# One scan over two states in a layer-0 Mamba scan, with the work around it moved

## The chip, the cores and the metric

The kernel runs on one NeuronCore of a Trainium2 chip, in one launch. The metric is the time of an execution on the device in microseconds (us). A core has a matrix engine (PE, with its weight loads shown as PEld), a vector engine (DVE), a scalar engine that evaluates functions (ACT), a general one (POOL) and DMA queues; each works through its own list of instructions in order and waits for the others by semaphores. All data here are 32-bit floats. [...]

## The reference

Four layers on an input of 2 x 256 x 48 x 48 (two batches of 2304 tokens, 256 channels). The first is a bidirectional Mamba layer, and the change is nearly all in it:

```python
def _selective_scan(u, delta, A, Bm, Cm, D):
    h0 = jnp.zeros((Bsz, d, A.shape[1]), u.dtype)
    def step(h, xs):
        d_t, B_t, C_t, u_t = xs
        dA = jnp.exp(d_t[..., None] * A)
        h = dA * h + (d_t * u_t)[..., None] * B_t[:, None, :]
        y = jnp.einsum('bdn,bn->bd', h, C_t)
        return (h, y)
    _, ys = lax.scan(step, h0, xs)
    return ys.transpose(1, 0, 2) + u * D

def _mamba_branch(xi, z, ...):
    xs = silu(conv4(xi) + conv_b)               # causal, per channel
    proj = xs @ xproj_w.T                       # 16 for dt, 16 B, 16 C
    dt = softplus(proj[..., :16] @ dtproj_w.T + dtproj_b)
    A = -exp(A_log)
    return _selective_scan(xs, dt, A, Bm, Cm, D) * silu(z)

h = layernorm(seq, ln_g, ln_b) + pos
xi, z = split(h @ in_proj_w.T)                  # 512 channels each
y = branch_f(xi, z) + flip(branch_b(flip(xi), flip(z)))
x = seq + y @ out_proj_w.T
```

So for each of 512 channels and each of 16 states there is a recurrence over 2304 tokens, in both directions, for two batches. Layer 1 is x + block(groupnorm(x)) with a linear attention, a depthwise convolution and an MLP. Layer 2 is an attention with 3 heads, where a head embeds tokens with `W_embed[h]` (768 x 256) and the heads' outputs go through `W_out` (256 x 768), then a graph-gated mixture of four experts. Layer 3 is an attention with sigmoid and a mixture of eight experts. Layers 2 and 3 normalise their tokens first.

## The kernel before

Channels lie on the partitions. The stream `E.xres` (128 x 2 x 4608) stays in SBUF over all layers. `layer0` cuts the 2304 tokens of a batch into 6 pieces of W = 384 and works through `order`: for each batch 6 pieces forward, then 6 backward, 24 in all. The 512 channels are DB = 4 blocks of 128.

For a piece, `prepare` makes what the scan needs: the 4-tap convolution as matmuls with diagonal weights (L266) with a copy out by ACT (L270), Silu (L276; in backward pieces also Silu of z, L278), the projection to dt, B and C (L286), which goes through DRAM as `bcd`, and dt as the softplus relu(v) + ln(1 + exp(-|v|)) with a correction for the rounding of 1 + e (L299 to L312). It ends with `dtu` = dt u on POOL (L314).

`scan` is the heart. For two channel blocks at a time and a group of GN = 4 states, B and C rows are loaded to all partitions (`bb`, `cc`, L354 and L356), POOL makes `db` = dt u B for the group and one block (128 x 1536, L359), and then for each state

- ACT computes exp(A dt) into a PSUM bank, tile `hs` (L376), 128 x 384;
- DVE runs the recurrence over it with `tensor_tensor_scan` (L382 forward, L385 backward, with reversed access), starting from `state` (0 in the first piece), in place in PSUM, or into an SBUF tile `ho` where the product goes to POOL;
- DVE (5 of 8) or POOL (3 of 8, `GP`) multiplies by C: `hc` (L390);
- ACT copies the last column to `state` (L392);
- PE adds `hc` to the sum over states by a matmul with the identity into `yp` (L344); products of POOL are added LAG = 4 states later.

PSUM in this stage: five banks for `hs` (tag "hs"), one for all other small products (`hold`, tag "mm"), two for `yp`.

Beside the scans of a piece, every two states, steps of three generators are issued: `project_out` of the piece before (backward pieces; L318 to L328, the last of which adds to `xres`), `prepare` of the next piece, and in pieces 0 to 9 `project_in` (normalisation, Sqrt L185, input projection) of a piece that is needed later. `beside` holds for each the number of its steps and the slot of 32 by which they are to end. What is issued is then put in order for each engine's queue by a scheduler. ACT's functions come from several tables; a change of table is an instruction of its own (ACT_TABLE_LOAD) on the line of the function that needs it.

Layer 1 begins with `group_norm` of batch 0 (L510 to L535): statistics (`bn_stats`, L517) over the stream, a matmul with `gmat` (L520, L528), which averages over groups of 8 channels, Sqrt, reciprocal, and the normalised tokens `xn` (L533); the first matmul with `wqkv` is L547. Layer 2's attention first makes products of weights for each of three heads: `w_eo` holds `W_embed[h]` beside `W_out` (L708, L709); 72 matmuls `pg` (L713) give `gm`, 144 small ones `pu` (L721) give `ub`; then come transposes of the tokens (L741) and the queries `pq` with `gm` (L750).

## Time and profile before

| | |
|---|---|
| median of 3 executions | 5455.18 us (5454.78 to 5460.61) |
| the profiled execution | 5416.49 us |
| its span | 5414.7 us |
| mean granted PE clock | 0.955 of full speed |
| PE / DVE / ACT / POOL busy over the span | 4771.7 / 3503.3 / 2365.8 / 2410.2 us |
| start of the first `dtu` / last scan's stage end | 92.2 / about 2393 us |
| first `pk` of layer 1 | 2417.2 us |
| first `pq` of layer 2 | 3181.6 us |

The profile comes from one execution, which was 0.7% shorter than the median of the three timed ones. A group's row gives line, engine, operation, output and inputs with shapes, the count, then busy time in us and the mean duration of one in ns, then the engine's idle time just before these instructions and what ended it. A timeline's row gives start and duration in us. Consecutive instructions of one engine overlap a little at their ends, so a busy mean is longer than the step from one start to the next.

### The profile page before, as it was taken

The numbers are of one execution on the slowest core, as the hardware profiler recorded it, in microseconds if no ns is written. First come the engines' busy times: TensorE is split into PE (matmuls) and PEld (weight loads), VectorE is DVE, ScalarE is ACT, GpSimd is POOL, SyncE is SP. The second block draws the span as 40 slices with busy tenths as digits, with TensorE's granted clock in tenths as the row PEclk, the third lists the DMA queues.
The fourth block names the chain that finished last, engine by engine and source line by source line (L and its number), as shares of the span: only waits on it lengthen the run. The fifth ranks groups of instructions, "written<-read, shape, count | busy, mean of one in ns | idle before, by whom it ended". The sixth has DMA issues, their size and how long they took to land. (4 is left out here: it accounts for less than half of the span.)

```text
span 5414.7 us, 47212 instructions
## 1 busy us (share of the span) xinstructions
PE 4771.7 (88%) x15246; PEld 2653.7 (49%) x15246; DVE 3503.3 (65%) x5360; ACT 2365.8 (44%) x4935; POOL 2410.2 (45%) x1308
## 2 busy tenths in 40 slices
PE   7888888888877778769999999999999999999897
PEld 3444444443333334335555555556654455555675
DVE  4899898898999898899996234447634401212343
ACT  5767777666667666632222213332123222222111
POOL 3888887788999888860000000008802100000321
PEclk8999999999999889989999989999999999999898
DMA  4445454443545444431110010011122200000422
GB/s 162 163 170 179 161 177 171 156 150 140 172 148 178 152 152 158 146 138 33 40 38 6 0 39 0 27 36 30 22 71 55 61 3 9 6 9 8 84 82 93
DMA packets 178083, 491.28 MB, mean 91 GB/s; under 512 B 32182, under 2 KB 100666, under 8 KB 177562
## 3 DMA queue, kind: packets, MB, share of 16 engines
q1 hardware_dynamic: 169114, 475.36, 25.6%
q0 software_dynamic: 8704, 12.73, 1.6%
q8 instruction: 124, 2.03, 0.2%
q14 instruction: 141, 1.16, 0.1%
HBM read 416.44 MB, written 71.58 MB: 90 GB/s over the span
## 5 line engine op out<-in xcount | busy, mean ns | idle before, releaser
L344 PE MATMUL yp<-hc,ident 128*128 128x384 f32 x3072 | 1203.1, 525 | 291.6 <-DVE hc L390 251.7
L359 POOL TENSOR_TENSOR db<-dtu,bb 128x1536 f32<-128x1536 f32 x384 | 1332.3, 3471 | 49.7 <-issue 19.1
L344 PEld LDWEIGHTS yp<-hc,ident 128*128 128x128 f32 x3072 | 577.1, 199 | 873.5 <-DVE hc L390 447.6
L390 POOL TENSOR_TENSOR hc<-ho,cc 128x384 f32<-128x384 f32 x576 | 579.4, 1014 | 185.3 <-DVE ho L382 83.3
L390 DVE TENSOR_TENSOR hc<-hs,cc 128x384 f32<-128x384 f32 x960 | 498.5, 540 | 39.1 <-PE yp L344 37.8
L376 ACT ACTIVATE hs<-dt,negab 128x384 f32<-128x384 f32 x768 | 434.2, 581 | 93.3 <-DVE ho L385 42.1
L376 ACT ACTIVATE hs<-dt,negaf 128x384 f32<-128x384 f32 x768 | 433.4, 581 | 55.0 <-DVE hc L390 25.5
L385 DVE TENSOR_TENSOR_SCAN hs<-hs,state,db 128x384 f32<-128x384 f32 x400 | 395.1, 1010 | 56.0 <-POOL db L359 30.3
L382 DVE TENSOR_TENSOR_SCAN hs<-hs,state,db 128x384 f32<-128x384 f32 x400 | 396.1, 1010 | 30.2 <-POOL db L359 22.9
L1771 POOL DMA_INDIRECT xe<-xt_d,token x48 | 47.4, 987 | 754.3 <-issue 716.0
L266 PE MATMUL mm<-xw,w_cv 128*128 128x384 f32 x768 | 287.5, 510 | 67.2 <-ACT xs L270 29.4
L1706 PE MATMUL po<-at,xtok 128*128 128x384 f32 x864 | 329.9, 507 | 7.7 <-ACT at L1704 7.5
L912 POOL PARTITION_ALL_REDUCE most<-most x1 | 0.4, 380 | 738.6 <-DVE most L911 738.6
L1697 PE MATMUL sp<-qT,xn 128*128 128x384 f32 x864 | 317.4, 487 | 0.0
L1704 ACT ACTIVATE at<-sp 128x384 f32<-128x384 f32 x216 | 104.6, 490 | 472.7 <-PE sp L1697 472.6
L1354 PE MATMUL ph<-xn,w 128*128 128x384 f32 x768 | 288.2, 519 | 19.3 <-ACT hid L1358 7.6
L627 PE MATMUL pf<-t,wfc 128*128 128x384 f32 x768 | 255.5, 489 | 0.0
L646 PE MATMUL po<-hid,wfc 128*128 128x384 f32 x768 | 253.6, 486 | 0.0
L385 DVE TENSOR_TENSOR_SCAN ho<-hs,state,db 128x384 f32<-128x384 f32 x240 | 240.0, 1000 | 15.2 <-ACT hs L376 15.1
L382 DVE TENSOR_TENSOR_SCAN ho<-hs,state,db 128x384 f32<-128x384 f32 x240 | 239.5, 998 | 8.4 <-ACT hs L376 8.2
L266 PEld LDWEIGHTS mm<-xw,w_cv 128*128 128x128 f32 x768 | 145.9, 196 | 195.1 <-ACT xs L270 46.9
L392 ACT COPY state<-hs 128x1 f32<-128x1 f32 x800 | 117.5, 155 | 278.2 <-DVE hc L390 276.3
(433 smaller groups left out, 7947.6 us busy)
## 6 DMA issues: line engine op xcount, KB each, us to landing
bb<-bcd SPq DMA_DIRECT2D x192, 768.0 KB, 4.1
cc<-bcd SPq DMA_DIRECT2D x192, 768.0 KB, 4.1
xw<-xi_d SPq DMA_DIRECT2D x24, 774.0 KB, 5.3
w<-in_m_w SPq DMA_DIRECT2D x16, 1024.0 KB, 5.8
y_d<-y SPq DMA_DIRECT2D x32, 384.0 KB, 2.3
ye<-y_d SPq DMA_DIRECT2D x32, 384.0 KB, 3.5
xi_d<-xz SPq DMA_DIRECT2D x48, 192.0 KB, 3.0
z_d<-xz SPq DMA_DIRECT2D x48, 192.0 KB, 3.2
```

The costliest lines, as they stand in the source:

```text
L266: nc.tensor.matmul(px, lhsT=w_cv[b, s][:, d * 4 + k, :], rhs=xw[:, d, o : o + W], start=k == 0, stop=k == 3,)
L344: nc.tensor.matmul(yp[d], lhsT=E.ident, rhs=hc, start=False, stop=summed[d] == NS)
L359: nc.gpsimd.tensor_tensor(db, bc(dtu[:, d, :], [P, GN, W], 1), bb, ALU.mult)
L376: nc.scalar.activation(hs, dt[:, d, :], AF.Exp, scale=nega[s][:, d * NS + n : d * NS + n + 1])
L382: nc.vector.tensor_tensor_scan(to, hs, db[:, j], init, ALU.mult, ALU.add)
L385: nc.vector.tensor_tensor_scan(to[:, ::-1], hs[:, ::-1], db[:, j, ::-1], init, ALU.mult, ALU.add)
L390: (nc.gpsimd if on_pool else nc.vector).tensor_tensor(hc, to, cc[:, j, :], ALU.mult)
L627: nc.tensor.matmul(pf, lhsT=wfc1[:, k, f * P : (f + 1) * P], rhs=t1[:, k, :], start=k == 0, stop=k == 1,)
L646: nc.tensor.matmul(po[m], lhsT=wfc2[:, f, m * P : (m + 1) * P], rhs=hid[:, i, :], start=f == 0, stop=f == 15,)
L1354: nc.tensor.matmul(ph, lhsT=w1[:, e, k, f * P : (f + 1) * P], rhs=xn[:, k, c * W : (c + 1) * W], start=k == 0, stop=k == 1,)
L1697: nc.tensor.matmul(sp, lhsT=xn[:, k, t0 + i * P : t0 + (i + 1) * P], rhs=qT[:, k, c * W : (c + 1) * W], start=k == 0, stop=k == 1,)
L1706: nc.tensor.matmul(po[m], lhsT=xtok[:, i, m * P : (m + 1) * P], rhs=at, start=i == 0, stop=i == MT - 1,)
```

## The change

**Two states in one scan.** The tile `hs` becomes two banks (128 x 1024), of which the columns 127 to 896 are used: twice 385 columns, 384 tokens and one leading column each (at the far end in backward pieces). `dt` gets a leading column of BIG = 1e25, so that exp(A dt) is 0 there, and A is kept below -2e-23; `db` gets a leading column too, which holds the state from the piece before (0 in a first piece). At the leading column the recurrence is thus begun anew, 0 times what came before plus the state, and one scan of 770 elements, started from an immediate 0, does two states. The exps stay one for each state, 128 x 385. The product with C is one instruction of 128 x 768 for the pair, on DVE or POOL in the same shares (`at * 3 % 8 >= 5`), the copy of the last columns is one of 128 x 2, and PE adds the two halves by two matmuls as before. The states are copied into `db` by ACT, 128 x 4 for a group. PSUM: two pair tiles `hs`, two banks for `mm`, two for `yp`. LAG is 2 pairs. The SBUF tiles `ho`, `hc` and `hcp` have two buffers of pairs where there were four of single states.

**dt u B mid-group.** `begin_group` issues the loads of `bb` and `cc`, the product `db` and the copy of the states half a group before they are used, also over the border to the next piece.

**dt.** The correction is rewritten, with one ACT instruction fewer for a piece, and `dtu` is four POOL instructions of one block each; `prepare` has 21 steps, to end at slot 29.

**Head products.** The products of layer 2's weights are made by `head_products`, beside the scans of the 12 pieces that follow the last `project_in` (there are 12 units of three steps), in the buffers of `pos`, `h`, `sq` and `rs`, which are free by then; the result goes to DRAM (`gm_d`) and is loaded again at the start of layer 2. `ub` stays in SBUF.

**Group norm.** `gmat` is built at the kernel's start, and `group_stats` of batch 0 runs beside the scans of the piece (1, "f", 1); that of batch 1 stays in layer 1. One normalisation in layer 3 gets a pool of its own.

```diff
-    GP = ((1, 3), (2,))
-    LAG = 4
+    LAG = 2
+    BIG = 1e25
...
-    psh = ctx.enter_context(tc.tile_pool(name="l0ps_h", bufs=5, space=PSUM))
-    ps = ctx.enter_context(tc.tile_pool(name="l0ps_s", bufs=1, space=PSUM))
+    psh = ctx.enter_context(tc.tile_pool(name="l0ps_h", bufs=2, space=PSUM))
+    ps = ctx.enter_context(tc.tile_pool(name="l0ps_s", bufs=2, space=PSUM))
...
-        dt = wp.tile([P, DB, W], F32, tag="dt", name="dt")
+        lead, body = (0, slice(1, W + 1)) if fwd else (W, slice(0, W))
+        dts = wp.tile([P, DB, W + 1], F32, tag="dt", name="dt")
+        nc.vector.memset(dts[:, :, lead : lead + 1], BIG)
+        dt = dts[:, :, body]
...
-        nc.scalar.activation(dtu, dtu, AF.Identity, bias=one[:, 1:2])
...
-        nc.vector.tensor_tensor(ex, ex, dtu, ALU.subtract)
+        nc.vector.scalar_tensor_tensor(ex, dtu, -1.0, ex, ALU.add, ALU.subtract)
         nc.vector.tensor_tensor(dt, dt, ln, ALU.add)
-        nc.vector.tensor_tensor(dt, dt, ex, ALU.add)
+        nc.vector.tensor_tensor(dt, dt, ex, ALU.subtract)
-        nc.gpsimd.tensor_tensor(dtu, dt, xs, ALU.mult)
+        for d in range(DB):
+            nc.gpsimd.tensor_tensor(dtu[:, d, :], dt[:, d, :], xs[:, d, :], ALU.mult)
+            yield
...
+    def head_products():
+        DT, D = 6, 768
+        for h, m, z in [(h, m, z) for h in range(3) for m in range(2) for z in range(2)]:
+            w_eo = []
+            for k in range(3):
+                rows = slice((z * 3 + k) * P, (z * 3 + k + 1) * P)
+                t = up.tile([P, 2, W], F32, tag=("pos", "h", "sq")[k], name="w_eo")
+                t = t.rearrange("p k w -> p (k w)")[:, : 2 * C]
+                nc.sync.dma_start(t[:, 0:C], p["W_embed"][h, rows, :])
+                nc.sync.dma_start(t[:, C:], p["W_outT"][rows, :])
+                w_eo.append(t)
+            yield
+            pg = ps.tile([P, 2 * C], F32, tag="mm", name="pg")
+            for k in range(3):
+                nc.tensor.matmul(
+                    pg, lhsT=w_eo[k][:, m * P : (m + 1) * P], rhs=w_eo[k], start=k == 0, stop=k == 2
+                )
+            if z == 0:
+                part = up.tile([P, 2 * C], F32, tag="rs", name="part")
+                nc.scalar.copy(part, pg)
+            else:
+                nc.vector.tensor_tensor(part, part, pg, ALU.add)
+                nc.sync.dma_start(E.gm_d[h, m], part)
+            yield
...
+    groups = [(d0, g, d) for d0 in range(0, DB, 2) for g in range(NS // GN) for d in (d0, d0 + 1)]
+    held = {}
+    def begin_group(q, first_piece, b, s, c, xs, y, dts, dtu, bcd):
+        d0, g, d = groups[q]
+        if d == d0:
+            for n, o in (("bb", 16), ("cc", 32)):
+                held[n] = wp.tile([P, GN, W], F32, tag=n, name=n)
+                nc.sync.dma_start(
+                    held[n], bcd[o + g * GN : o + (g + 1) * GN, :].partition_broadcast(P)
+                )
+        lead, body = (0, slice(1, W + 1)) if s == "f" else (W, slice(0, W))
+        db = wp.tile([P, GN, W + 1], F32, tag="db", name="db")
+        nc.gpsimd.tensor_tensor(
+            db[:, :, body], bc(dtu[:, d, :], [P, GN, W], 1), held["bb"], ALU.mult
+        )
+        if first_piece:
+            nc.gpsimd.memset(db[:, :, lead : lead + 1], 0.0)
+        else:
+            nc.scalar.copy(db[:, :, lead], state[:, d, g * GN : (g + 1) * GN])
+        return db, held["cc"]
...
+            for j in range(0, GN, 2):
+                n = g * GN + j
+                on_pool = at * 3 % 8 >= 5
+                hs = psh.tile([P, 1024], F32, tag="hs", name="hs")[:, 511 - W : 513 + W]
+                for i in range(2):
+                    o = d * NS + n + i
                     nc.scalar.activation(
-                        hs, dt[:, d, :], AF.Exp, scale=nega[s][:, d * NS + n : d * NS + n + 1]
+                        hs[:, i * (W + 1) : (i + 1) * (W + 1)], dts[:, d, :], AF.Exp,
+                        scale=nega[s][:, o : o + 1],
                     )
...
+                nc.vector.tensor_tensor_scan(
+                    to[:, way], hs[:, way],
+                    db[:, j : j + 2, :].rearrange("p i w -> p (i w)")[:, way], 0.0, ALU.mult, ALU.add,
+                )
+                to = to.rearrange("p (i w) -> p i w", i=2)
+                hc = wp.tile([P, 2, W], F32, tag="hcp" if on_pool else "hc", name="hc")
+                (nc.gpsimd if on_pool else nc.vector).tensor_tensor(
+                    hc, to[:, :, body], cc[:, j : j + 2, :], ALU.mult
+                )
+                if step < NCH - 1:
+                    nc.scalar.copy(state[:, d, n : n + 2], to[:, :, last])
...
+                if j == 0:
+                    if q + 1 < len(groups):
+                        begun = begin_group(q + 1, step == 0, b, s, c, xs, y, dts, dtu, bcd)
+                    elif following:
+                        begun = begin_group(0, step == NCH - 1, *following)
...
-            beside.append((prepare(nb, s2, c2, ready), 15, 25))
+            beside.append((prepare(nb, s2, c2, ready), 21, 29))
         if i < len(pieces):
             beside.append((project_in(*pieces[i]), 12, 32))
+        elif i < len(pieces) + 12:
+            beside.append((islice(heads, 3), 3, 32))
+        if (b, s, step) == (1, "f", 1):
+            beside.append((group_stats(E, up, lambda: hold()[:, 0:2], 0), 15, 32))
```

## The prediction

> **What bounds the kernel now.** I read the page first: its engine table, its 40 slices, and its groups of instructions. In the slices
>
> ```profile
> PE   7888888888877778769999999999999999999897
> ...
> DVE  4899898898999898899996234447634401212343
> ...
> POOL 3888887788999888860000000008802100000321
> ```
>
> slices 2 to 18 (135 us each) are another regime than the rest: DVE is at 8 to 9 tenths and POOL just behind. That is layer 0. After it PE is the bound and this change touches only two spots there. I then took the busy times over the scan stage; the columns are PE, PEld, DVE, ACT, POOL, the clock, the DMA share and GB/s:
>
> ```profile
> 100.00:2393.00 2293.00, 1856.97 (x5000) 918.80 (x5001) 2079.73 (x2684) 1550.77 (x3575) 1960.04 (x984) 0.95 0.46 160
> 1527.20:1616.60 89.40, 71.53 (x193) 33.55 (x192) 86.67 (x108) 61.94 (x155) 82.56 (x41) 0.98 0.45 159
> 1901.10:1997.90 96.80, 78.95 (x210) 40.64 (x210) 87.44 (x118) 65.86 (x157) 82.12 (x43) 0.91 0.43 156
> ```
>
> DVE works 2079.7 of 2293 us (91%), so the stage goes as DVE's work plus DVE's holes: 213 us of holes over 24 pieces, 9 each. The second line is one forward piece of batch 1 (2.7 us of holes), the third a backward one (9.4). POOL works 82 us in each, ACT 62 to 66. What DVE's time is made of, by shape:
>
> ```profile
> L390 DVE TENSOR_TENSOR hc<-hs,cc 128x384 f32<-128x384 f32 x960 | 498.5, 540 | 39.1 <-PE yp L344 37.8
> L382 DVE TENSOR_TENSOR_SCAN hs<-hs,state,db 128x384 f32<-128x384 f32 x400 | 396.1, 1010 | 30.2 <-POOL db L359 22.9 <-ACT hs L376 6.9
> ...
> L382 DVE TENSOR_TENSOR_SCAN hs<-hs,db 128x384 f32<-128x384 f32 x80 | 74.6, 951 | 21.4 <-POOL db L359 16.2 <-ACT hs L376 4.3 <-ACT state L392 0.9
> ...
> L177 DVE TENSOR_TENSOR h<-xres,mm 128x768 f32<-128x768 f32 x12 | 11.4, 947 | 29.6 <-PE mm L176 18.0 <-PE mm L202 11.6
> ...
> L1599 DVE TENSOR_TENSOR_SCAN run<-ones,before,tot 128x18 f32<-128x18 f32 x8 | 1.4, 247 | 0.0
> ```
>
> Busy times overlap at the ends, so I price by the step from start to start in DVE's timeline. A table change on ACT (here for the Silu of z) stands in ACT's timeline, and what DVE lost to it in DVE's:
>
> ```profile
> 2236.28 0.58 ACT L376 ACTIVATE hs<-dt,negab 128x384 f32<-128x384 f32 x1
> ...
> 2237.38 1.28 ACT L278 ACT_TABLE_LOAD   x1
> 2238.67 1.49 ACT L278 ACTIVATE y<-y 128x1536 f32<-128x1536 f32 x1
> ...
> 2241.16 1.28 ACT L376 ACT_TABLE_LOAD   x1
> 2242.45 0.58 ACT L376 ACTIVATE hs<-dt,negab 128x384 f32<-128x384 f32 x1
> ```
>
> ```profile
> 2230.57 1.01 DVE L385 TENSOR_TENSOR_SCAN ho<-hs,state,db 128x384 f32<-128x384 f32 x1
> 2231.49 1.00 DVE L385 TENSOR_TENSOR_SCAN hs<-hs,state,db 128x384 f32<-128x384 f32 x1
> ...
> 2238.45 1.02 DVE L385 TENSOR_TENSOR_SCAN hs<-hs,state,db 128x384 f32<-128x384 f32 x1 [0.49 <-POOL db L359]
> 2239.39 1.47 DVE L390 TENSOR_TENSOR hc<-hs,cc 128x384 f32<-128x384 f32 x3
> 2243.07 1.02 DVE L385 TENSOR_TENSOR_SCAN hs<-hs,state,db 128x384 f32<-128x384 f32 x1 [2.21 <-ACT hs L376]
> ```
>
> A scan takes a step of 0.915; three products take 1.47, so one 0.46 by steps (busy 0.54). ACT began no exp from 2236.28 to 2242.45, 6.2 us; DVE, with up to five exps in store, lost 2.2 of them.
>
> **Paired scans.** A pair on DVE is now 2 x 0.915 + 2 x 0.46 = 2.75; a pair whose product goes to POOL costs DVE 2 x 0.915 = 1.83. The paired scan has 770 elements and an immediate start. Between the scan of 18 (247 ns, L1599) and that of 384 (1010) an element costs (1000-247)/366 = 2.06 ns; from 951 for the immediate form the pair is 951 + 386 x 2.06 = 1746, and less the 95 ns by which steps overlap 1.65. The product pair is the 768 form of L177: 947, a step of 0.865 by one overlap of 0.08. So a DVE pair costs 2.52 and saves 0.23, a POOL pair saves 0.175. There are 24 x 32 = 768 pairs, 480 and 288: 110 + 50 = 160. In the four first pieces the scans already start from an immediate and save 0.11 less on 128 pairs: 14. Together **-146**, 6.1 a piece. Bounds: a pair at 2 x 0.915 takes 134 of it back; at the slope of the scans of 384 read down to 1.9 ns an element it gives 50 more.
>
> **Two pair buffers where five banks were.** That is the price. The store in front of DVE falls to one pair, 1.65 to 2.52 us of work, and the exps of pair k+2 wait for the product (or, for POOL pairs, the scan) of pair k. A burst is 1.28 + 1.48 + 1.28 = 4.04, and then two exps (0.58 each) and a state copy before the next scan: 5.2 between two pairs. Walking ACT's and DVE's queues of the changed order with these durations, in a backward piece of batch 1: Silu of z falls between the two exps of one pair, DVE stands 5.2; Silu of xs 3.2; Abs and Relu 1.2; Exp and Identity 0.4; Ln 0.4; sum 10.4 where 9.4 stand: +1.0. Forward batch 1, whose holes are 2.7, has no Silu of z, so Silu of xs and part of the rest: +1.5. With project_in's Sqrt beside (pieces 1 to 9) a hole of about 3 more: forward batch 0 +5.7, backward batch 0 +3. Six pieces of each: 6 x 11.2 = **+67**. Below, -100: the holes now charged to POOL db (74 in the waits) and to yp could go, since db is begun half a group earlier. Above, +322: three full bursts a piece, 15.6, less the 2.2 that DVE now waits for ACT's exps (52 in its waits over 24 pieces), 13.4 a piece. I take the walk, as it is nearest to the real order, but I walked some twenty pairs of 768.
>
> **What else is in the pieces.** DVE gets the bn_stats of batch 0 (12 of 0.55, step 0.46, and eight small ones) +7; the head products' adds (6 of 128x512 at 0.69 and 18 small at 0.2) +8 to 10; the start of layer 0, with two tiles instead of five and the dtu in four, +3: **+20**. ACT loses an Identity of 1.57 per piece and gains 16 state copies of 0.19 in front of db; they wait for the last scan of the older db, which lies behind on DVE, so cost exps at most 0.2 each. POOL: 16 db of 3.47, 12 product pairs of 1.90 (the 128x768 product of L1412 on POOL, mean 1897), four dtu of about 1.0: 82.3 a piece, as before; a forward piece of 89.4 - 6.1 + 1.5 = 84.8 still lies above it. PE takes 72 pg (512 columns, 0.52 each) and 144 pu, 61 us, at 81% use: hidden, and if each head unit held up the conv matmuls on their two banks by 1 us, +12. SP issues 72 weight loads and 6 stores more, in a stage at 46% of DMA; bb and cc are issued half a group early, ahead of the head loads. If SP held them back a group by 2 us once a piece, +24.
>
> **Layer 2's start.** In PE's timeline the first head matmul starts at 3118.1, the last ends at 3178.6 and the first pq is at 3181.6:
>
> ```profile
> 3118.14 5.25 PE L721 MATMUL pu<-vec,w_eo 128*128 128x1 f32 x24 [2.50 <-DMA w_eo<-in_W_embed]
> ...
> 3170.79 7.82 PE L721 MATMUL pu<-vec,w_eo 128*128 128x1 f32 x48
> ...
> 3181.60 6.38 PE L750 MATMUL pq<-xn,gm 128*128 128x384 f32 x16
> ```
>
> Without them pq comes when the last norm (its last matmul runs 3123.25 to 3124.9) and the transposes beside it are through, about 3124.5: **-57** (-63 to -50). The gm reload (three loads, 1.57 MB) can be issued early and is about the size that lands in 6 us (w, 1 MB, 5.8); uncovered it costs those 6.
>
> **Layer 1's start.** From the last xres add (2398.75) to the first pk (2417.16) are 18.4 us: mask, stats, two small matmuls, xn. With batch 0's statistics done only xn (2.85) and the load of wqkv (landing 4.7 after) stay, about 8: **-10** (-13 to -8).
>
> **Sum:** -146 + 67 + 20 - 57 - 10 = -126, on an execution of 5416.5 (span 5414.7, 1.8 around it). That execution lies 38.7 (0.7%) under the median of 5455.2; I apply the difference to the median: **5330**.
>
> **A rule against it.** In the burst above the Silu starts 1.29 after its load started, and the load lasts 1.28: nothing more lies between. The Trainium skill's "ScalarE: Activation LUTs", section "What ACT_TABLE_LOAD costs", gives 1283 ns for a load and about 1380 more for a drain, 2.66 per switch. With one pair in store every such drain would fall on DVE: by that page an estimate of three bursts of two switches in 24 pieces, 199 us more, and the change would be slower, about 5530. The row decides: no drain.
>
> **Rivals.** (A) *The two buffers starve DVE.* Each burst stalls it nearly whole. For: ACT's bursts are three a piece, and today's 2.2 in the burst shown was lost with five banks. Against: my walk, where the store of one pair still covers half. It decides when a piece gets over 193/24 = 8.0 us more holes (193 = 146 + 57 + 10 - 20); halfway to the bound of 13.4, at 10.7, it ends 5455 - 193 + 257 = **5519** (5584 at the bound). (B) *No more holes than today*, because the early db removes the 74 us of db waits: 5455 - 193 = **5262**; POOL's 82.3 x 24 = 1975 does not yet forbid that. (C) *The scans gain nothing*, since new holes of 6.1 a piece eat the 146: only heads, layer 1 and the +20 stay, 5455 - 47 = **5408**. A pair that costs two single scans, with the walk's holes, would be 5330 + 134 = 5464, about no change.
>
> **How the numbers follow.** Chances: forecast 0.50 (own range 5290 to 5375), B 0.13, C 0.15, A 0.19, and 0.03 that gains and stalls meet within 0.2%, about what a measurement of this kernel can tell from no change. Faster 0.78, slower 0.19. The range 5240 to 5470 takes in B, C and the near end of A; it leaves out the rest of A, some 0.15, and 0.04 below.
>
> **What would show it.** Scans of 128x770 at about 1.75 and products of 128x768 near 0.95 on DVE; DVE at 1.95 ms busy in a scan stage near 2240; its holes charged to ACT hs, no longer to POOL db; the longest near 5 where Silu of z runs; POOL at 82 a piece. First pq some 57 earlier against the end of layer 1, first pk 8 after the last xres add. Wrong if: the pair costs over 1.8, ACT's waits exceed 10 a piece in all four kinds of piece, a queue that I called free (SP, PE's two banks) shows up as releaser, or layer 2 waits for gm.

## The result and the profile after

The changed kernel takes 5517.35 us (median of 4, 5510.46 to 5519.21) against 5456.7 for the kernel before in the same comparison: a ratio of 1.0108, interval 1.009 to 1.0125. It is 61 us slower. The forecast was 5330, 126 us faster than before; the range ended at 5470. So the sign was wrong and the time lay outside the range.

The two traces can be laid side by side at four marks (start of the trace to the start of the last `xres` add of layer 0, from there to the first `pk`, from there to the first `pq`, from there to the end; us):

| stretch | before | after | difference |
|---|---|---|---|
| to the last `xres` add | 2398.8 | 2529.5 | +130.7 |
| to the first `pk` of layer 1 | 18.4 | 6.1 | -12.3 |
| to the first `pq` of layer 2 | 764.4 | 706.7 | -57.7 |
| to the end | 2233.1 | 2271.7 | +38.6 |

The last row is not the change: whatever was done to layer 0, that stretch took 2223 to 2232 us in the traces whose comparison gave the kernel before 5404 to 5413 us, and 2268 to 2277, at a lower granted PE clock (0.951 to 0.955 in it for 0.957 to 0.963), where it gave 5456 to 5457; the trace of before, with 2233, goes with the first. Times below are therefore told as ratios to the kernel before run beside them, or by the first mark. Without the last row the traces differ by 130.7 - 12.3 - 57.7 = 60.7 us, close to the measured 61.

The start of PE's work in the two layers behind, in PE's timeline of the changed kernel:

```profile
2535.61 4.91 PE L653 MATMUL pk<-wqkv,xn 128*128 128x512 f32 x6 [6.16 <-DVE sc L617]
...
3242.34 7.41 PE L833 MATMUL pq<-xn,gm 128*128 128x384 f32 x16 [4.32 <-issue]
```

These are the two gains that the forecast had as -10 and -57: -12.3 and -57.7. All of the error lies in the scan stage, which was to become 59 us shorter (-146 + 67 + 20) and ends 131 later. Its slices, and its times from the first scan to the last add, then for one backward piece of batch 1 (stretch, its length, busy PE, PEld, DVE, ACT and POOL with their instructions, clock, DMA share, GB/s):

```profile
PE   7878878878777778878999999999699999999897
...
DVE  3888888888888878889998334446454411212343
...
POOL 2787787778788887882000000018602200000331
```

```profile
110.50:2529.90 2419.40, 1937.35 (x5232) 992.38 (x5232) 2055.76 (x1513) 1534.91 (x3240) 1924.79 (x830) 0.93 0.45 156
```

```profile
2013.20:2112.60 99.40, 83.48 (x233) 43.17 (x231) 82.94 (x65) 64.05 (x137) 81.02 (x37) 0.93 0.47 162
```

DVE's 9s became 8s. Its work fell from 2085.8 us (in the same stretch before) to 2055.9, and its holes, the time in which it does nothing, grew from 214 to 364. The groups show that the parts were priced well one by one, 1.75 for a scan of 770 and 0.95 for a product of 768:

```profile
L496 DVE TENSOR_TENSOR_SCAN hs<-hs,db 128x770 f32<-128x770 f32 x480 | 840.8, 1756 | 186.8 <-ACT hs L490 132.3 <-POOL db L434 40.7 <-POOL db L438 9.2
L496 DVE TENSOR_TENSOR_SCAN ho<-hs,db 128x770 f32<-128x770 f32 x288 | 503.9, 1750 | 83.2 <-ACT hs L490 66.6 <-POOL db L434 15.3 <-ACT state L506 0.6
L502 DVE TENSOR_TENSOR hc<-hs,cc 128x768 f32<-128x768 f32 x480 | 454.9, 952 | 49.4 <-PE yp L459 19.4 <-DVE hs L496 0.5 <-issue 0.4
```

The waits for ACT's exps are 132.3 + 66.6 = 199 us. Before they were 52, in DVE's waits over the same stage (us in total, times, longest):

```profile
DVE ho L385 <- ACT hs L376: 18.7, 14, 2.9
DVE hs L385 <- ACT hs L376: 13.1, 14, 2.3
DVE hs L382 <- ACT hs L376: 11.2, 11, 2.2
DVE ho L382 <- ACT hs L376: 9.3, 12, 1.7
```

The waits for POOL's `db` are 65, where they were 74. One burst, that is a stretch in which ACT is busy with table loads and a long function and makes no exps, in ACT's and in DVE's timeline:

```profile
2055.73 0.58 ACT L490 ACTIVATE hs<-dt,negab 128x385 f32<-128x385 f32 x1
2056.33 1.28 ACT L317 ACT_TABLE_LOAD   x1
2057.62 1.49 ACT L317 ACTIVATE y<-y 128x1536 f32<-128x1536 f32 x1
2059.01 0.14 ACT L506 COPY state<-hs 128x2 f32<-128x2 f32 x1
2059.17 1.28 ACT L490 ACT_TABLE_LOAD   x1
2060.47 0.58 ACT L490 ACTIVATE hs<-dt,negab 128x385 f32<-128x385 f32 x1
```

```profile
2053.84 1.76 DVE L496 TENSOR_TENSOR_SCAN ho<-hs,db 128x770 f32<-128x770 f32 x1 [0.15 <-ACT hs L490]
2055.52 0.93 DVE L502 TENSOR_TENSOR hc<-hs,cc 128x768 f32<-128x768 f32 x1
2061.14 1.77 DVE L496 TENSOR_TENSOR_SCAN hs<-hs,db 128x770 f32<-128x770 f32 x1 [4.69 <-ACT hs L490]
```

The first exp of a pair is written before the Silu of z, the second behind it, and DVE, which has finished all it had, stands 4.69 us (the prediction had 5.2 for this place). That the Silu starts 1.29 after its load agrees with the row that the prediction went by. The other thing to see is in the steps of DVE's timeline, a little earlier:

```profile
2038.96 1.76 DVE L496 TENSOR_TENSOR_SCAN hs<-hs,db 128x770 f32<-128x770 f32 x1
2040.63 0.54 DVE L466 TENSOR_TENSOR y<-yp,y 128x384 f32<-128x384 f32 x1
...
2044.06 1.76 DVE L496 TENSOR_TENSOR_SCAN hs<-hs,db 128x770 f32<-128x770 f32 x1
2045.86 0.96 DVE L502 TENSOR_TENSOR hc<-hs,cc 128x768 f32<-128x768 f32 x1
```

From a scan to an instruction that doesn't need it the step is 1.67 (2038.96 to 2040.63); to the product of this same scan it is 1.80 here and 1.85 in the median of 308 such steps without another wait. With five banks another scan or product nearly always stood between a scan and its own product (all but 8 of 960); with two tiles the product came at once in 312 of 480.

### The profile page after: what moved, and what is told of

The parts are those of the page before. It is cut to its first block, busy times and chain, and to the rows that moved or that the text cites. A ratio compares the mean times of both kernels' runs of the same rounds, so it can differ in the third digit from the quotient of the medians.

```text
span 5514.0 us, 45247 instructions
## 1 busy us (share of the span) xinstructions
PE 4797.1 (87%) x15246; PEld 2679.1 (49%) x15246; DVE 3459.3 (63%) x4147; ACT 2347.0 (43%) x4596; POOL 2368.1 (43%) x1156
## 5 line engine op out<-in xcount | busy, mean ns | idle before, releaser
L496 DVE TENSOR_TENSOR_SCAN hs<-hs,db 128x770 f32<-128x770 f32 x480 | 840.8, 1756 | 186.8 <-ACT hs L490 132.3
L502 POOL TENSOR_TENSOR hc<-ho,cc 128x768 f32<-128x768 f32 x288 | 512.8, 1781 | 332.2 <-PE yp L459 116.4
L496 DVE TENSOR_TENSOR_SCAN ho<-hs,db 128x770 f32<-128x770 f32 x288 | 503.9, 1750 | 83.2 <-ACT hs L490 66.6
L502 DVE TENSOR_TENSOR hc<-hs,cc 128x768 f32<-128x768 f32 x480 | 454.9, 952 | 49.4 <-PE yp L459 19.4
L490 ACT ACTIVATE hs<-dt,negab 128x385 f32<-128x385 f32 x768 | 444.8, 585 | 79.8 <-DVE hc L502 51.6
L490 ACT ACTIVATE hs<-dt,negaf 128x385 f32<-128x385 f32 x768 | 441.0, 582 | 48.0 <-DVE hc L502 31.7
L1441 ACT ACTIVATE hid<-ph,vec 128x384 f32<-128x384 f32 x192 | 110.3, 580 | 338.2 <-PE ph L1437 240.3
L1790 PEld LDWEIGHTS po<-at,xtok 128*128 128x128 f32 x864 | 149.7, 189 | 177.5 <-ACT at L1788 109.0
L1452 PE MATMUL po<-hid,w 128*128 128x384 f32 x512 | 176.9, 496 | 46.0 <-ACT hid L1441 44.5
L1781 PEld LDWEIGHTS sp<-qT,xn 128*128 128x128 f32 x864 | 161.6, 190 | 105.2
```

The costliest lines, as they stand in the source:

```text
L490: nc.scalar.activation(hs[:, i * (W + 1) : (i + 1) * (W + 1)], dts[:, d, :], AF.Exp, scale=nega[s][:, o : o + 1],)
L496: nc.vector.tensor_tensor_scan(to[:, way], hs[:, way], db[:, j : j + 2, :].rearrange("p i w -> p (i w)")[:, way], 0.0, ALU.mult, ALU.add,)
L502: (nc.gpsimd if on_pool else nc.vector).tensor_tensor(hc, to[:, :, body], cc[:, j : j + 2, :], ALU.mult)
L1452: nc.tensor.matmul(po, lhsT=w2[:, e, f, m * P : (m + 1) * P], rhs=hid[:, f, :], start=f == 0, stop=f == FT - 1,)
L1781: nc.tensor.matmul(sp, lhsT=xn[:, k, t0 + i * P : t0 + (i + 1) * P], rhs=qT[:, k, c * W : (c + 1) * W], start=k == 0, stop=k == 1,)
L1790: nc.tensor.matmul(po[m], lhsT=xtok[:, i, m * P : (m + 1) * P], rhs=at, start=i == 0, stop=i == MT - 1,)
```

## The experiments

Theory 1: the loss is in the pairing. Two pair tiles leave too little work in front of DVE when ACT is away, and put each product right behind its own scan. Rival 1: the work moved into the pieces lengthens them. Rival 2: the mid-group `db` and the rewritten dt do. The table gives each run's ratio to the kernel before beside it, the start of the last `xres` add, and from the first scan to that add's end DVE's busy time, its holes, and its waits for ACT's exps before scans (us). PSUM, in which the exps lie, is the memory that PE writes its sums to; ACT and DVE work in it too, while POOL's instructions in these traces have no tile there.

| run | ratio, interval | last add | DVE busy | holes | waits for exps |
|---|---|---|---|---|---|
| before | 1 | 2398.8 | 2085.8 | 214 | 52 |
| changed | 1.0108 (1.009, 1.0125) | 2529.5 | 2055.9 | 364 | 199 |
| 1 moves only | 0.9938 (0.9921, 0.9955) | 2429.6 | 2098.7 | 229 | 44 |
| 2 single scans | 0.9924 (0.9907, 0.994) | 2430.4 | 2136.8 | 196 | 36 |
| 3 three pair tiles, shared | 1.0653 (1.0635, 1.067) | 2817.2 | 2027.8 | 688 | 438 |
| 4 changed, one table | 0.9904 (0.9887, 0.992) | 2412.4 | 2032.9 | 275 | 116 |
| 5 single scans, one table | 0.9865 (0.9848, 0.9881) | 2403.4 | 2139.1 | 172 | 40 |
| 6 POOL's pairs in SBUF | 1.1078 (1.106, 1.1097) | 3052.7 | 2355.8 | 591 | 148 |
| 7 product free of its scan | 1.0882 (1.0864, 1.09) | 2952.8 | 2378.1 | 469 | 30 |
| 8 single scans, four banks | 0.9971 (0.9959, 0.9984) | 2445.6 | 2120.2 | 228 | 66 |
| 9 single scans, three banks | 1.0065 (1.0048, 1.0082) | 2503.2 | 2131.1 | 269 | 93 |
| 10 single scans, old dt | 0.9949 (0.9932, 0.9965) | 2431.7 | 2100.1 | 231 | 44 |
| 11 three pairs end to end | 1.2214 (1.2191, 1.2236) | 3674.5 | 2080.4 | 1449 | 1208 |
| 12 no copies of states | 1.0019 (1.001, 1.0029) | 2477.6 | 2024.5 | 345 | 141 |

### 1. The moves alone

The changed kernel with `scan`, `prepare` and the PSUM pools of the kernel before; head products, `group_stats` and `gmat` stay where the change puts them.

```diff
-    psh = ctx.enter_context(tc.tile_pool(name="l0ps_h", bufs=2, space=PSUM))
+    psh = ctx.enter_context(tc.tile_pool(name="l0ps_h", bufs=5, space=PSUM))
...
-        begun = scan(step, beside, begun, ready, *now)
+        scan(step, beside, *now)
```

> The kernel before with only the moves: head products beside the scans, group statistics of batch 0 beside the scans, gmat at the start; single scans in five banks, db at the group's start and the old dt as before. Theory 1 (the loss is in the pairing: two buffers make DVE wait for ACT, and each product stands right behind its own scan): the two starts gain what the trace showed, 57.7 (first pk to first pq) and 11.5 (last xres add to first pk), the added work in the pieces costs 20 at most: 5385 to 5405. Rival 1 (the moved work is what lengthens the scan stage, the pairing is innocent): the stage grows by most of its 131, so 5457 - 69 + 80 to 131 = 5468 to 5519.

Measured: 0.9938, 31 us less than the 5404 beside it, 5373 where theory 1 had 5385 to 5405: the gain was larger than expected. The stage ends 31 us later than before, not 20, and the two starts gain 70 (6.9 from the last add to `pk`, 706 from there to `pq`): -39 by the trace. Rival 1 falls: of the 131 us, 31 are the moved work.

### 2. Single scans, everything else of the change

Single scans in five banks for the exps and one for the small products, from the state's pointer, as before.

```diff
-                hs = psh.tile([P, 1024], F32, tag="hs", name="hs")[:, 511 - W : 513 + W]
...
+                hs = psh.tile([P, W], F32, tag="hs", name="hs")
...
+                    nc.vector.tensor_tensor_scan(to, hs, db[:, j], init, ALU.mult, ALU.add)
...
-                    db[:, j : j + 2, :].rearrange("p i w -> p (i w)")[:, way], 0.0, ALU.mult, ALU.add,
```

> The changed kernel with single scans in five banks, from the state's pointer, as before; db mid-group, the rewritten dt and the moves stay. Theory 1: 5360 to 5420: the moves' gain, up to 60 of the 74 us that DVE waited for db, less up to 46 for the dt operations, which took 8.06 us a piece on DVE in the changed kernel and 6.16 before. Rival 1: within 20 of the changed kernel's 5517. Rival 2 (mid-group db and the new dt are what costs, through DVE and POOL working on the same data at the same time): 5440 or more, with the dt operations still at 8 us a piece.

Measured: 0.9924, 39 us less, 5366 within theory 1's 5360 to 5420. The last add comes within 1 us of the first experiment's, so mid-group `db` and the new dt together do nothing to the stage, although the dt operations take 37 us more of DVE's time (176 against 139). Its line over the scan stage, DVE third:

```profile
97.70:2431.00 2333.30, 1935.71 (x5240) 973.92 (x5240) 2136.84 (x2742) 1532.25 (x3564) 1980.76 (x1056) 0.94 0.46 162
```

Against it the paired kernel differs by the pairing and what belongs to it: the PSUM tiles, a second bank for small products, the leading columns and the copies into `db`. It has 81 us less work on DVE and 167 more holes, begins its scans 13 later and ends the stage 99 later. Of the 167, 163 are waits for exps; some 28 are the short gaps, too short to count as waits, between a scan and its own product; other waits fell. DVE's waits for PE are 44 in the paired kernel and 54 here, so the lower PE clock in the paired kernel's stage (0.93 against 0.94) is no rival. Rival 2 falls, and the loss is in the pairing.

### 3. A third pair tile that the small products share

```diff
-    psh = ctx.enter_context(tc.tile_pool(name="l0ps_h", bufs=2, space=PSUM))
-    ps = ctx.enter_context(tc.tile_pool(name="l0ps_s", bufs=2, space=PSUM))
+    psh = ctx.enter_context(tc.tile_pool(name="l0ps_h", bufs=3, space=PSUM))
...
-        if scanning:
-            return ps.tile([P, 512], F32, tag="mm", name="mm")[:, :W]
         return psh.tile([P, 1024], F32, tag="hs", name="mm")[:, :W]
...
```

> The changed kernel with three pair tiles in PSUM instead of two; the small products, which had two banks of their own, take theirs from the same three. Theory 1: DVE's waits for ACT's exps fall from 199 to about 100 and scans are less often followed by their own product (1.85 us a step against 1.67, some 330 times, 60 us): 5370 to 5440. Against it works that a small product now occupies a whole pair tile; if that weighs as much, 5500. Rival 1 or 2: no change beyond 20, 5497 to 5537.

Measured: 1.0653, a miss for every expectation. ACT's timeline shows exps behind a tile that a small product holds (here that of `project_out`, until DVE adds it to `xres`):

```profile
1515.52 1.20 ACT L487 ACTIVATE hs<-dt,negaf 128x385 f32<-128x385 f32 x2
1518.70 1.20 ACT L487 ACTIVATE hs<-dt,negaf 128x385 f32<-128x385 f32 x2 [1.98 <-DVE xres L371]
```

The waits for exps rose to 438. A small product takes its turn in the ring of tiles, so the exps wait for its reader, which itself waits in DVE's or ACT's queue. This made the store in front of DVE smaller, not larger, and can't count as a test of a third tile.

### 4 and 5. No changes of ACT's tables, with pairs and with single scans

Silu, Ln and Sqrt of layer 0 become Relu, so the values are others; 4 table loads are left in the stage of each, where the changed kernel has 139.

```diff
-        nc.scalar.activation(xs, xs, AF.Silu)
+        nc.scalar.activation(xs, xs, AF.Relu)
...
-        nc.scalar.activation(ln, dtu, AF.Ln)
+        nc.scalar.activation(ln, dtu, AF.Relu)
...
```

> The changed kernel with Silu, Ln and Sqrt of layer 0 replaced by Relu, so that its output is another and layer 0 needs no change of ACT's tables: bursts of 4.04 become 1.48. Theory 1: the 199 us of waits for exps fall to 60 to 90, the time to 5380 to 5420. Rival (the waits for exps come from the exps themselves, 2 x 0.58 behind a free tile, not from the bursts): 5480 or more.

> The single scans of the second experiment with Silu, Ln and Sqrt of layer 0 replaced by Relu: another output, no changes of table in layer 0. In the paired kernel that took 117 us from the scan stage. Theory 1 (only the two pair buffers make a burst of ACT cost DVE time): singles gain 20 to 50, the 31 to 40 us of waits for exps that they have. Rival (the bursts cost any version about the same, since ACT's work is on the path): singles gain 90 or more. Before minus 60 to 90 by theory 1, before minus 130 or less by the rival.

Measured: 0.9904 and 0.9865. The last add comes 117 us earlier with pairs (2529.5 to 2412.4), 27 earlier with single scans (2430.4 to 2403.4). Pairs came out lower than expected (5353 for 5380 to 5420), although their waits for exps fell less far (116, not 60 to 90); single scans lie where theory 1 had them (73 under the kernel before, for 60 to 90). This is the decisive pair: the same table changes cost the paired kernel 90 us more than the single one, of the 99 that it lost. The two lines over the scan stage, pairs first:

```profile
104.90:2413.00 2308.10, 1897.14 (x5228) 977.92 (x5228) 2032.92 (x1512) 1369.03 (x3110) 1923.28 (x831) 0.94 0.46 164
```

```profile
93.30:2404.00 2310.70, 1922.11 (x5234) 969.19 (x5234) 2139.12 (x2741) 1375.32 (x3433) 2012.73 (x1056) 0.95 0.47 164
```

They show also what is left: without table changes pairs have 106 us less work on DVE and 104 more holes, so pairing still gains next to nothing. It waits 116 us for exps where single scans wait 40. What ACT does between exps there is the remaining functions of 1.5 us each and the copies; which of them costs how much was not tested here.

### 6. The pairs of POOL out of SBUF

ACT writes the exps of POOL's pairs into the SBUF tile `ho`, and their scans run there in place; this was to give four buffers.

```diff
-                hs = psh.tile([P, 1024], F32, tag="hs", name="hs")[:, 511 - W : 513 + W]
+                if on_pool:
+                    hs = wp.tile([P, 2 * (W + 1)], F32, tag="ho", name="ho")
+                else:
+                    hs = psh.tile([P, 1024], F32, tag="hs", name="hs")[:, 511 - W : 513 + W]
...
-                to = wp.tile([P, 2 * (W + 1)], F32, tag="ho", name="ho") if on_pool else hs
+                to = hs
```

> The changed kernel, but ACT writes the exps of the pairs whose product POOL makes into the SBUF tile (two buffers, there already) in which their scan then runs in place; the two PSUM pair tiles are left to the other 5 of 8 pairs. So four buffers stand before DVE instead of two. Theory 1: the 199 us of waits for exps fall to 60 to 100 and a product can be put behind another pair's scan: 110 to 170 less than the changed kernel, that is before minus 50 to before minus 110. Rival (not the buffers but the extra work and the pair's own order cost the time; or a scan out of SBUF is slower than out of PSUM, by 0.2 us or more in 288 scans): within 40 of the changed kernel, before plus 20 or more.

Measured: 1.1078, outside every expectation. The scans out of SBUF take 2935 ns in the mean, those out of PSUM 1753 as ever:

```profile
L499 DVE TENSOR_TENSOR_SCAN ho<-ho,db 128x770 f32<-128x770 f32 x288 | 844.6, 2935 | 310.8 <-POOL db L434 242.3 <-POOL db L438 60.8 <-ACT db L440 4.7
L499 DVE TENSOR_TENSOR_SCAN hs<-hs,db 128x770 f32<-128x770 f32 x480 | 834.2, 1753 | 162.5 <-ACT hs L493 145.8 <-POOL db L434 10.8 <-POOL db L438 3.2
```

and one of them, in DVE's timeline, beside POOL's:

```profile
2013.98 3.22 DVE L499 TENSOR_TENSOR_SCAN ho<-ho,db 128x770 f32<-128x770 f32 x1 [0.88 <-POOL db L434]
```

```profile
2013.91 1.67 POOL L505 TENSOR_TENSOR hc<-ho,cc 128x768 f32<-128x768 f32 x1
```

POOL's product had begun 0.07 earlier and ended at 2015.58. The scan is recorded with 3.22 = 1.60 to that end and 1.62 behind it, about a scan's own step of 1.67: it was held until POOL's product was through. The Trainium skill, "SBUF — State Buffer", section "SBUF: two separate sides", states it so: a DVE instruction with two SBUF inputs and a GpSimd (POOL) instruction that reads SBUF contend for one pair of ports, and whichever comes first has it for its whole length. The traces here agree with it for scans (2935 against 1753 ns in the mean) and, in the next experiment, for products. The experiment therefore added 288 x 1.18 = 340 us of another loss; the waits for exps are 148, but whether four buffers would have cured them stays untold by it.

### 7. A product that doesn't read its scan

```diff
-                    hc, to[:, :, body], cc[:, j : j + 2, :], ALU.mult
+                    hc, (to if on_pool else db[:, j : j + 2, :])[:, :, body], cc[:, j : j + 2, :], ALU.mult
```

> The changed kernel with DVE's product multiplying C with db instead of with the scan's result: another output, the same instructions in size and number; a product no longer waits for its own scan, and the PSUM tile is free after the scan and not after the product. If the step of 1.85 us between a scan and its own product (1.67 elsewhere) is a wait for the scan's results, it goes to 1.67: 330 x 0.18 = 60 less busy and idle time of DVE; the tile comes free 0.87 earlier, which takes another 40 to 90 from the waits for exps. Together 100 to 150 less than the changed kernel: before minus 40 to minus 90. If the step stays at 1.85, it belongs to the change from scan to product, and only the earlier release counts: before plus 20 to minus 30.

Measured: 1.0882, again a miss in the total: the product now has both inputs in SBUF and takes 1673 ns in the mean:

```profile
L502 DVE TENSOR_TENSOR hc<-db,cc 128x768 f32<-128x768 f32 x480 | 800.6, 1673 | 92.8 <-POOL db L434 41.7 <-PE yp L459 38.7 <-POOL db L438 12.3
```

That is 480 x 0.72 = 346 us more. The waits for exps fell to 30 us, but ACT had that much more time for them, so this is no price of the earlier release. The disputed step can be read nonetheless, as here:

```profile
1648.21 1.76 DVE L496 TENSOR_TENSOR_SCAN hs<-hs,db 128x770 f32<-128x770 f32 x1
1649.88 0.94 DVE L502 TENSOR_TENSOR hc<-db,cc 128x768 f32<-128x768 f32 x1
```

From a scan in PSUM to its own pair's product it is 1.67 in the median of 161, as to any other instruction. So the 1.85 of the changed kernel is a wait for the scan's own results, 0.18 us each, and with 308 such steps (those with no other wait) 55 us.

### 8 and 9. Single scans with four and with three banks

```diff
-    psh = ctx.enter_context(tc.tile_pool(name="l0ps_h", bufs=5, space=PSUM))
+    psh = ctx.enter_context(tc.tile_pool(name="l0ps_h", bufs=4, space=PSUM))
```

and `bufs=3` in the ninth.

> The single scans of the second experiment with four banks for the exps instead of five: the same PSUM space as two pair tiles, in single states. Theory 1 in its narrow form (the store in front of DVE in time is what counts, whatever its grain): four single exps are three ready scans behind the one at work, 2.7 us and more, against one pair's 1.67 to 2.5: the waits for exps, 31 to 40 us with five, grow by 20 to 60, the time likewise: before minus 20 to plus 20. Rival (any loss of a bank costs as much as the pairing did, 99 us): before plus 40 or more. Rival (the grain alone does it): no change, before minus 30 to 45.

> The same with three banks: two ready scans behind the one at work, 1.8 us, near what one waiting pair is. Theory 1: the waits for exps reach those of the paired kernel, about 200, so 130 to 180 more than with five banks: before plus 90 to plus 140 (single scans keep their dearer steps). If the time stays below before plus 30, the store in front of DVE is not what the pairing lost.

Measured: 0.9971 and 1.0065; the last add comes 15 and 73 us later than with five banks, the waits for exps go from 36 to 66 and 93. DVE's waits, with four banks and then with three:

```profile
DVE hs L478 <- ACT hs L472: 28.0, 24, 2.9
DVE ho L481 <- ACT hs L472: 15.9, 12, 2.6
DVE hs L481 <- ACT hs L472: 14.3, 17, 2.4
DVE ho L478 <- ACT hs L472: 7.8, 9, 2.1
```

```profile
DVE hs L481 <- ACT hs L472: 37.0, 28, 2.9
DVE hs L478 <- ACT hs L472: 30.1, 20, 2.9
DVE ho L478 <- ACT hs L472: 15.8, 10, 3.0
DVE ho L481 <- ACT hs L472: 10.0, 8, 3.0
```

The first is at the low end of the expectation, the second below it (+36 against the kernel before where +90 to +140 was expected). So the store in front of DVE does set its waits, with nothing else changed. But two pairs, in the same four banks, do worse (199) than four single exps (66) and than three (93), so the size of the store alone does not explain the pairing's loss: the grain, or something else that comes with pairs, matters too. A likely reason, not shown, is that a pair tile comes free only when both its states are through and is ready only when both its exps are; and the copies into `db` are in the paired kernel alone (experiment 12).

### 10. Single scans mid-group with the old dt

```diff
-        nc.vector.scalar_tensor_tensor(ex, dtu, -1.0, ex, ALU.add, ALU.subtract)
+        nc.vector.tensor_tensor(ex, ex, dtu, ALU.subtract)
```

with the second Identity on ACT, `dtu` as one instruction and `prepare`'s steps spread as before.

> The second experiment's kernel with the dt operations and the one dtu instruction of the kernel before. Its three dt operations took 7.35 us a piece on DVE against 5.8 with the old form in the first experiment; 24 x 1.5 = 37 us if that comes from the rewriting. If it comes from where they fall beside POOL's work (both inputs in SBUF: in the sixth and seventh experiments scans and products of that kind took up to 4.9 us instead of 1.75 and 0.94 while POOL was at work), the old form takes as long in the new place, and the time stays within 15 of the second's, before minus 25 to 55; otherwise before minus 60 to 80.

Measured: 0.9949, 14 us above the second experiment by the ratios, whose intervals overlap; the last add is within 1.3 us. The three dt operations are back at 5.8 us a piece (139 us in all against 176), so the longer times come with the rewritten form and its spread, which were not taken apart. But the stage gains nothing from it: DVE's work is 37 us less and its holes 35 more, most of that before the second dt operation (L351), where it waits 39 us for ACT's Ln and copies of states against 10 in experiment 2. Of the expectation, the shorter operations were the one side's and the unchanged time the other's.

### 11. Three pairs end to end in five banks

```diff
+    banks = psh.tile([P, 5 * 512], F32, name="banks")
+    turn = [0]
...
-                hs = psh.tile([P, 1024], F32, tag="hs", name="hs")[:, 511 - W : 513 + W]
+                turn[0] += 1
+                o = turn[0] % 3 * 2 * (W + 1)
+                hs = banks[:, o : o + 2 * (W + 1)]
```

> The changed kernel with a third pair tile and nothing else taken from the small products' own place: three pairs of 770 columns lie end to end in five banks (so some exps write across a bank's border, and two pairs can share a bank), the small products have one bank as before the change, the sums two. Theory 1: the waits for exps fall from 199 to 60 to 100, and where a scan stands between a scan and its product the step is 1.67 again: the stage is 120 to 170 shorter than the changed kernel's, before minus 60 to before minus 110, faster than single scans. Rival (the third tile doesn't help, as ACT itself is late, or sharing banks slows the engines): changed kernel within 40, before plus 20 or more.

Measured: 1.2214, outside every expectation. As slices of one tile the three places were not kept apart: in the trace a pair's exps begin only when the pair before has been scanned, multiplied and its last columns copied, and DVE stands about 1.5 us before nearly every scan:

```profile
3030.17 1.20 ACT L497 ACTIVATE banks<-dt,negab 128x385 f32<-128x385 f32 x2
3034.37 0.16 ACT L513 COPY state<-banks 128x2 f32<-128x2 f32 x1 [3.00 <-DVE hc L509]
3034.56 1.20 ACT L497 ACTIVATE banks<-dt,negab 128x385 f32<-128x385 f32 x2
```

```profile
3031.46 1.77 DVE L503 TENSOR_TENSOR_SCAN banks<-banks,db 128x770 f32<-128x770 f32 x1 [1.57 <-ACT banks L497]
```

That is the pairing with no store at all: 1145 us more than with two tiles. It bounds the effect. Three pair tiles of their own, a bank for the small products and two for the sums would make nine banks, one more than either kernel lays out; that was not tried.

### 12. No copies of states on ACT

Every piece begins from zero; the 640 copies out of the scans and the 320 copies into `db` are left out.

```diff
-        if first_piece:
+        if True:
             nc.gpsimd.memset(db[:, :, lead : lead + 1], 0.0)
...
-                if step < NCH - 1:
+                if False:
                     nc.scalar.copy(state[:, d, n : n + 2], to[:, :, last])
```

> The changed kernel without any copy of states on ACT: every piece begins from zero (POOL sets the leading columns), so the output is another; 640 copies of 128x2 and 320 of 128x4 are gone from ACT's queue, 171 us of its work, among them those that stand in the queue in front of the exps and wait for a scan. Theory 1 (two tiles and bursts): the exps still wait for the tiles, so the stage loses 10 to 40: before plus 20 to plus 50. Rival (the copies into db hold back the exps queued behind them, which the prediction put at 0.2 us each and no more): 60 to 110 less, before plus 0 to minus 50.

Measured: 1.0019, and a last add 52 us earlier; the waits for exps fall from 199 to 141, those for POOL's `db` rise from 65 to 90. The time lies between the two expectations: 10 above the kernel before, where theory 1 had 20 to 50 and its rival 0 to -50. The copies are a second part of ACT's lateness; single scans have copies out of the scans too (1280 of them), so not all of the 52 belongs to the pairing.

## Why the prediction was wrong

By its own steps (us):

| step | forecast | measured |
|---|---|---|
| paired scans, DVE's work | -146 | -81 (changed kernel against experiment 2) |
| two pair buffers, holes | +67 | +167 (the same comparison); +150 against the kernel before |
| what else is in the pieces | +20 | +31 (experiment 1); mid-group `db` and dt: +1; first scan 13 later than in experiment 2 |
| layer 2's start | -57 | -57.7 |
| layer 1's start | -10 | -12.3 |

The first three make 131, -81 + 167 + 31 + 1 + 13. Two steps failed: the price of the two pair buffers was put at less than half of what it is, and the gain of the paired scans at nearly twice. For the buffers the size was wrong and not the mechanism; for the paired scans a wait was missing.

**Paired scans.** The durations were right: 1.75 and 0.95, with steps of 1.67 where 1.65 was forecast, and 0.87. Part of the difference is a slip: the slope was worked out with 1000 ns for a single scan where the row beside it has 1010, and with that the pair comes to 1756, as measured. What failed is that the step was taken from rows where a scan is followed by something that doesn't need it. With two tiles its own product often follows it, at 1.85: 55 us, half of it in DVE's busy time and half in gaps. With 27 from there, 0.02 of the step on 768 scans (15) and the dt operations, which took 194 us and not 176 (17), nearly all of the 65 is found. The forecast had the rewritten dt at nothing on DVE, where it was 148 before.

**Two pair buffers.** The mechanism was named and its single places priced well: behind Silu of z 4.69 for 5.2, behind Silu of xs 3.40 for 3.2. What was mis-sized is the sum over the kinds of piece. Holes in the six pieces of each kind, where a piece goes from its first scan to the next piece's:

| kind of piece | before | changed | more | forecast |
|---|---|---|---|---|
| forward, batch 0 | 47 | 80 | +33 | +34 |
| backward, batch 0 | 68 | 96 | +28 | +18 |
| forward, batch 1 | 34 | 92 | +58 | +9 |
| backward, batch 1 | 65 | 96 | +31 | +6 |

That is 150 for 67, and 74 of the missing 83 are in batch 1. (The moves alone, experiment 1, add 15 to the holes, 4 in the forward and 11 in the backward pieces of batch 1.) Its forward pieces were put at "+1.5" each, from one piece with 2.7 us of holes and because they have no Silu of z. They had the fewest holes before and got the most: their waits for ACT's exps are 10.4 a piece, in the other kinds 7.4 to 7.9. The copies into `db`, put at "at most 0.2 each" and then not entered in the sum, are among what the twelfth experiment took out for 52.

**The rivals.** A, the starving of DVE, is what happened, but that its 5519 lies next to the measured 5517 is luck: the holes grew by 6.2 a piece over those of the kernel before ((364 - 214) / 24), less than the 8.0 that A needed, and this sufficed because DVE's work fell by 30 us and not by 126. B's reason fell too: the waits for `db` went from 74 to 65, not to nothing, and experiment 2, with `db` just as early and single scans, has 73. C had new holes of 6.1 a piece, and they came; but it set them against a gain of 146. Its mechanism, gain and holes cancelling, is what is left without table changes (experiments 4 and 5: -106 and +104).

**The rule weighed.** The table load has no drain behind it here (1.29 from the load's start to Silu's, as before), so the change was slower for another reason than that rule would have given; that the estimate by it, about 5530, lies near the measured time is luck.

What stays open: why pairs wait longer for exps than single scans in the same four banks or fewer, and how much a true third pair tile would give. Experiments 3, 6 and 11 were meant to show the latter and each brought a loss of its own.

## What to carry to other kernels

Where an engine is the bound, what feeds it has to be in store for as long as the feeder can be away: count the burst (here 4 us of table loads and a Silu) against the work that the buffers hold, for every kind of stage, the one with the fewest holes most of all. Merging two instructions halves the number of buffers in the same space and leaves less room to put other work between a producer and its consumer; the step to a dependent instruction is not the step to an independent one (here 1.85 and 1.67). The moves without the pairing (experiments 1 and 2) are 0.6 to 0.8% faster than the kernel before, and beat both kernels.

## What the runs showed of the hardware

- DVE instructions with two inputs in SBUF were held by a running POOL instruction (experiments 6 and 7): scans of 1.75 us took up to 4.99 and products of 0.94 up to 4.19, while the scans with one input in PSUM kept their time in the same run (1.73 to 1.77 in 480). That speaks for keeping the exps in PSUM.
- A scan followed by its own product costs 0.18 us more than one followed by anything else (1.85 and 1.67).
- A change of ACT's table costs its load, 1.28 us, and nothing behind it: the next function starts 1.30 us after the load's start in the median of the changed kernel's 245 loads, and 1.29 in the burst shown.
